# A macaron block on one core: the feed-forward bias by accumulating DMA instead of GpSimd adds

## The chip, the cores and the metric

The kernel runs on one core of a Trainium2 chip. A core has five engines with an instruction queue each: TensorE (PE, matmuls; PEld is its weight load), VectorE (DVE), ScalarE (ACT), GpSimd (POOL) and SyncE (SP), which here only issues transfers. Each queue is worked through in order; engines wait for each other through semaphores. Sixteen DMA engines move data between DRAM and the on-chip memory SBUF, whichever queue has issued the transfer. The metric is the device time of one execution in microseconds; less is better.

## What is computed

The input x has 2 sequences of 1024 rows of 1024 numbers, float32. A block runs over it: half a feed-forward network, causal attention with 32 query and 8 key/value heads of 32, and half a feed-forward network again, each on the layer-normalised rows and each added to x:

```
x = x + 0.5 * ffn(layernorm(x))
x = x + attn(layernorm(x))
x = x + 0.5 * ffn(layernorm(x))

def ffn(x):
    w_full = softmax over the 2 largest of 8 gate logits x @ gate_w.T, 0 elsewhere
    result = einsum('bsd,od->bso', x, base_w) + base_b
    low = einsum('bsd,erd->ebsr', x, lora_A)
    lora_out = einsum('ebsr,eor,bse->bso', low, lora_B, w_full)
    return result + 2.0 * lora_out
```

What matters here is `base_b`: a vector of 1024 numbers, half of which is added to every row of x twice, once in each of the two networks. Both networks have the same weights.

## The kernel before, in words

**Tiles.** The 2048 rows are 16 tiles of 128 rows. A tile of x, named xt, is 128 x 1024 float32, 512 KB in SBUF, one row to a partition. It is loaded once (L126), changed in place by both networks and the attention, and stored (L748, L750). Every dense product is made of three float16 products, high by high, high by low and low by high parts (L358 to L360), 512 columns of output at a time, in one of two PSUM buffers named pd.

**Stages of one tile.** `stage_a1` is the first network, `stage_a2` the keys, values and queries, `unit_s1` and `unit_s2` the attention of one group of heads (L573 score matmuls for the row maxima L590, then L712 scores, L718 exponentials, L636 sums of pairs, L657 products with the values), `stage_c1` the output projection, `stage_c2` the second network. Before each dense stage `layernorm` makes the normalised tile xn (L349, ScalarE), splits it into the halves hl (L310, L311), and transposes them through DMA into tt (L314). Queries are transposed by DMA too (qt, L553), twice for each pair of groups. The weights of the attention stay in DRAM as prepared halves and are streamed, 1 MB per load, into three buffers ws (L370); the weights wb of the networks stay in SBUF.

**The network** (`ffn`, L390) does this for its tile: 24 matmuls of gate and low-rank input into psa; two GpSimd adds (L395), one for each half of the columns, of the bias tile bb to xt; gate logits and routing in small VectorE steps (L400 to L418); then for each half of 512 columns 24 base matmuls, three low-rank matmuls (L440 to L442), and one VectorE instruction (L444) that scales the PSUM and adds it to xt. The two adds have to come after xn has been made, which reads xt without the bias, and before L444 of the same columns. `layernorm` also uses GpSimd, for two instructions on one number per row (L335, L337).

**The bias tile.** bb is 128 x 1024 float32 in SBUF. One SyncE transfer in the preparation (L793) reads the 4 KB of the bias once for every partition, and ScalarE halves it (L233).

**Order.** The preparation, up to about 130 us, is written out by hand: loads, scales (`pow2`, with a GpSimd power at L177), splits, and the first networks of tiles 0 to 2. `pin` keeps its SyncE transfers in program order. After it, dense work and attention are interleaved by `step` according to `plan`: in a usual step the second network of tile s-2, the output projection of s-1, keys and queries of s+1, the first network of s+2. Tile 8 (`LATE`) does its attention last, so its second network is the end of the kernel. Apart from pinned transfers, the order on each engine is laid out by a scheduler with a timeline of its own when the kernel is built, by the dependencies and by when operands are expected.

Of the kernel before, what the change touches and what calls it, by code (L numbers as in the profile page):

```python
# [9 lines left out]
FP = mybir.dt.float32  # L10
# [3 lines left out]
ALU = mybir.AluOpType  # L14
AX = mybir.AxisListType

B, T, D = 2, 1024, 1024
NH, NKV, DH, GRP = 32, 8, 32, 4
E, R = 8, 16
P = 128  # L20
KB = D // P
# [18 lines left out]
def kernel(  # L40
# [16 lines left out]
    nc = tc.nc  # L57
# [3 lines left out]
    const = ctx.enter_context(tc.tile_pool(name="const", bufs=1))  # L61
    wres = ctx.enter_context(tc.tile_pool(name="wres", bufs=1))
    small = ctx.enter_context(tc.tile_pool(name="small", bufs=SB))
# [4 lines left out]
    dram = ctx.enter_context(tc.tile_pool(name="dram", bufs=1, space=bass.MemoryType.DRAM))  # L68
# [17 lines left out]
        out=cmask, in_=cmask, compare_op=ALU.is_ge, fill=-NEG, base=0,  # L86
# [6 lines left out]
        out=tri, in_=tri, compare_op=ALU.is_gt, fill=0.0, base=0,  # L93
# [7 lines left out]
    nc.gpsimd.memset(ones, 1.0)  # L101
    cosT = const.tile([P, TPB, DH // 2], FP)
    sinT = const.tile([P, TPB, DH], FP)
    bb = const.tile([P, D], FP)

    qst = [stat.tile([P, NH, P], HP, name=f"qst{j}") for j in range(2)]
    kst = stat.tile([P, NKV, P], HP)
# [9 lines left out]
    def pin(ins):  # L117

        if pinned[0]:
            tc.keep_in_program_order(ins)  # L120
# [3 lines left out]
    def load_x(t):  # L124
        xt = xp.tile([P, D], FP, name="xt")
        pin(nc.sync.dma_start(out=xt, in_=late["x"] if t == LATE and late else xf[bass.ts(t, P), :]))  # L126
        xts[t] = xt
# [97 lines left out]
    def prep_lora(st):  # L225
        c = const.tile([P, 2], FP, name="sl")
        nc.vector.tensor_copy(c[:, 0:1], S["l",])
        nc.vector.scalar_tensor_tensor(c[:, 1:2], INV["b", 0], S["l",], S["b", 1], ALU.mult, ALU.mult)
        for n in range(2):
            h, s = bass.ts(n, 512), c[:, n : n + 1]  # L230
            nc.scalar.activation(lbh[:, h], st[:, h], AF.Copy, scale=s)
            nc.vector.scalar_tensor_tensor(lbl[:, h], st[:, h], s, lbh[:, h], ALU.mult, ALU.subtract)
        nc.scalar.mul(bb, bb, 0.5)  # L233

    KV = [wk_in, wv_in]
    CHUNKS = {
# [8 lines left out]
    def stage(ci, h, slot, eng):  # L245
        staged[ci, h] = piece(slot, CHUNKS[ci][0], h, eng)
# [81 lines left out]
    def layernorm(xt, n=1):  # L328
        st = small.tile([P, 2, 6], FP, name="bst")
        for c in range(2):  # L330
            nc.vector.bn_stats(st[:, c, :], xt[:, bass.ts(c, 512)])
        mv = small.tile([P, 2], FP, name="mv")
        nc.vector.bn_aggr(mv, st.rearrange("p a b -> p (a b)"))
        ve = small.tile([P, 1], FP, name="ve")
        nc.gpsimd.tensor_scalar(ve, mv[:, 1:2], EPS, None, ALU.add)  # L335
        r = small.tile([P, 1], FP, name="r")
        nc.gpsimd.tensor_tensor(r, ve, mhalf, ALU.pow)  # L337
        n1 = small.tile([P, 1], FP, name="n1")
        nc.vector.scalar_tensor_tensor(n1, ve, r, r, ALU.mult, ALU.mult)
        nc.vector.tensor_scalar(n1, n1, -0.5 * XS, 1.5 * XS, ALU.mult, ALU.add)  # L340
        rs = small.tile([P, 1], FP, name="rs")
        nc.vector.tensor_tensor(rs, n1, r, ALU.mult)
        nb = small.tile([P, 1], FP, name="nb")
        nc.vector.scalar_tensor_tensor(nb, mv[:, 0:1], -1.0, rs, ALU.mult, ALU.mult)
        xn = fpool.tile([P, D], FP, name="xn")
        sp = Split(n)
        for i in range(n):
            c = bass.ts(i, D // n)
            nc.scalar.activation(xn[:, c], xt[:, c], AF.Identity, bias=nb, scale=rs)  # L349
            sp.add(xn)  # L350
        return sp

    def dense(ps, tt, wsel, n=512, last=True):

        for k in range(KB):
            wh, wl = wsel(k)
            th, tl = tt.high(k), tt.low(k)
            nc.tensor.matmul(ps, lhsT=th, rhs=wh, start=(k == 0), stop=False)  # L358
            nc.tensor.matmul(ps, lhsT=th, rhs=wl, start=False, stop=False)  # L359
            nc.tensor.matmul(ps, lhsT=tl, rhs=wh, start=False, stop=(last and k == KB - 1))  # L360
            if k % 2 == 1:
                yield
# [27 lines left out]
    def ffn(xt, tt, done):  # L390
        psa = p_dense.tile([P, 512], FP, name="pd")
        yield from dense(psa[:, 0 : P + E], tt, lambda k: (ag[:, 0, k, :], ag[:, 1, k, :]))
        for n in range(2):
            c = bass.ts(n, 512)
            nc.gpsimd.tensor_tensor(xt[:, c], xt[:, c], bb[:, c], ALU.add)  # L395

        lg = small.tile([P, E], FP, name="lg")
        nc.scalar.activation(lg, psa[:, P : P + E], AF.Copy, scale=S["cg"])
        nv = small.tile([P, 1], FP, name="nv")
        nc.vector.tensor_reduce(nv, lg, AX.X, ALU.max, negate=True)  # L400
        ex = small.tile([P, E], FP, name="ex")
        nc.scalar.activation(ex, lg, AF.Exp, bias=nv)
        fe = lg.unsqueeze(1).to_broadcast([P, E, E])
        ee = lg.unsqueeze(2).to_broadcast([P, E, E])
        lw = small.tile([P, E, R], FP, name="lw", bufs=1)
        gt, eq = lw[:, :, 0:E], lw[:, :, E : 2 * E]
        nc.vector.tensor_tensor(gt, fe, ee, ALU.is_gt)
        nc.vector.tensor_tensor(eq, fe, ee, ALU.is_equal)
        nc.vector.tensor_tensor(eq, eq, tri, ALU.mult)
        nc.vector.tensor_tensor(gt, gt, eq, ALU.add)  # L410
        rk = small.tile([P, E], FP, name="rk")
        nc.vector.tensor_reduce(rk, gt, AX.X, ALU.add)
        nc.vector.scalar_tensor_tensor(ex, rk, 1.5, ex, ALU.is_lt, ALU.mult)
        sm = small.tile([P, 1], FP, name="sm")
        nc.vector.tensor_reduce(sm, ex, AX.X, ALU.add)
        nc.vector.reciprocal(sm, sm)
        nc.vector.tensor_scalar(ex, ex, sm, S["inva2"], ALU.mult, ALU.mult)
        nc.vector.tensor_tensor(  # L418
            lw, psa[:, 0:P].rearrange("p (e r) -> p e r", r=R),
            ex.unsqueeze(2).to_broadcast([P, E, R]), ALU.mult,  # L420
        )
        yield True
        psb = [None, None]
        lh = ll = None
        for n in range(2):
            ps = p_dense.tile([P, 512], FP, name="pd")
            psb[n] = ps
            yield from dense(
                ps, tt, lambda k: (wb[:, n, 0, k, :], wb[:, n, 1, k, :]), last=False
            )  # L430
            if n == 0:
                pst = p_s1.tile([P, GRP, P], FP, name="s1")[:, 0, :]
                nc.tensor.transpose(pst, lw.rearrange("p e r -> p (e r)"), ident)
                lh = small.tile([P, P], HP, name="lh", bufs=LB)
                ll = small.tile([P, P], HP, name="ll", bufs=LB)
                nc.scalar.copy(lh, pst)
                nc.vector.tensor_tensor(ll, pst, lh, ALU.subtract)
                yield
            c = bass.ts(n, 512)
            nc.tensor.matmul(ps, lhsT=lh, rhs=lbh[:, c], start=False, stop=False)  # L440
            nc.tensor.matmul(ps, lhsT=lh, rhs=lbl[:, c], start=False, stop=False)
            nc.tensor.matmul(ps, lhsT=ll, rhs=lbh[:, c], start=False, stop=True)  # L442
            yield
            nc.vector.scalar_tensor_tensor(xt[:, c], ps, S["uf", n], xt[:, c], ALU.mult, ALU.add)  # L444
            done(n)
            if n == 0:
                yield True

    def stage_a1(t):
        tt = layernorm(xts[t])  # L450
        yield

        def done(n):
            if n == 1:
                Ts["x2", t] = layernorm(xts[t])
                if t == LATE:
                    late["x"] = dram.tile([P, D], FP, name="xlate")
                    nc.sync.dma_start(out=late["x"], in_=xts.pop(t))

        yield from ffn(xts[t], tt, done)  # L460
        yield True
# [310 lines left out]
    for h in range(2):  # L772
        for src, c in ((a_in, slice(0, P)), (g_in, slice(P, P + E))):
            pin(
                nc.sync.dma_start(
                    out=agst[:, h, :, c],
                    in_=src[h * (D // 2) : (h + 1) * (D // 2), :].rearrange("(k p) n -> p k n", p=P),
# [4 lines left out]
    pin(nc.sync.dma_start(out=lst, in_=lb_in))  # L782
    b0 = [piece(h - 2, [wb_in[:, 0:512]], h, nc.sync) for h in range(2)]
    load_x(1)
    a1 = [stage_a1(t) for t in range(3)]
    next(a1[0])
    prep_gate(gst)
# [2 lines left out]
    prep_base(0, b0)  # L790
    load_x(2)
    next(a1[1])
    pin(nc.sync.dma_start(out=bb, in_=bias_in.partition_broadcast(P)))  # L793
    stage(2, 0, 0, nc.scalar)
    stage(2, 1, 1, nc.scalar)
    prep_base(1, b1)
    prep_lora(lst)
    stage(3, 0, 2, nc.sync)
    stage(3, 1, 5, nc.sync)
# [240 lines left out]
```

## Time and profile before

| | us |
|---|---|
| three runs of the kernel before: median | 1523.7 |
| lowest and highest of them | 1520.88 and 1530.89 |
| the profiled execution, in all | 1528.72 |
| its span, first to last instruction | 1527.0 |

The page of a profile gives, for one execution, the busy time of each engine, the same in 40 slices of equal length (38 us here; each digit is the busy share in tenths), the DMA queues, the chain of work that ended last, and the costliest groups of instructions. A group's line has line, engine and operation, output and input with shapes and count, then busy time and mean of one, then the engine's idle time just before them and what ended it. The chain is followed back from the last instruction, at each step to what released it: its shares say which engine or transfer ended the waits, not how busy each was. Queries of the trace give the instructions in order of time, the minimum, median and maximum of one line, what waited for what, and the sums over chosen windows.

### The profile page before, as it was taken

What the parts mean: (1) busy time and instruction counts of PE and PEld (TensorE: products, weight loads), DVE (VectorE), ACT (ScalarE), POOL (GpSimd) and SP (SyncE); (2) the same over time, 40 slices, a digit from 0 to 9 for tenths busy, and PEclk for the clock granted to TensorE, in tenths of its full rate; (3) what the DMA queues carried; (4) which work ended last, traced back from release to release, by engine and by line L of the source; (5) the groups of instructions that cost most, each with busy time, mean ns of one, the idle gap of its engine ahead of it and who ended that gap; (6) DMA issues with size and microseconds to landing.
All of it is one profiled execution on the core that took longest, in us unless ns stands there. A gap on an engine that the chain in (4) does not pass through costs nothing.

```text
span 1527.0 us, 35303 instructions
## 1 busy us (share of the span) xinstructions
PE 1404.1 (92%) x14548; PEld 783.4 (51%) x14548; DVE 1139.7 (75%) x2420; ACT 755.5 (49%) x1374; POOL 450.1 (29%) x665
## 2 busy tenths in 40 slices
PE   3686897989999999999999899999999999989998
PEld 2243444455555555555654445555555555556544
DVE  6877656686968879789764767886869788689753
ACT  7564334453545545456552434553545455556631
POOL 3443213432323233122121323332323232312231
PEclk9798999989999999999999999999999999999999
DMA  9957697658575581853646769857383853834651
GB/s 274 333 156 204 115 237 205 206 127 264 123 238 137 153 254 31 235 160 69 209 160 191 216 161 272 202 160 234 72 294 69 237 147 70 271 69 98 133 170 45
DMA packets 293075, 267.30 MB, mean 175 GB/s; under 512 B 258480, under 2 KB 261552, under 8 KB 272432
## 3 DMA queue, kind: packets, MB, share of 16 engines
q1 hardware_dynamic: 289360, 252.45, 60.5%
q10 hardware_dynamic: 3552, 12.58, 2.3%
q8 instruction: 114, 1.87, 0.5%
q14 instruction: 49, 0.40, 0.1%
HBM read 181.63 MB, written 20.45 MB: 132 GB/s over the span
## 4 chain that ended last, share of the span: by engine, by line
PE 65%; DVE 13%; DMA 13%; ACT 3%; issue 2%; POOL 1%; SPq 1%; DVEq 0%; ACTq 0%; POOLq 0%
PE pd L358 13%; PE pd L359 13%; PE pd L360 13%; PE av L657 10%; PE s L712 7%; PE s L573 6%; DMA ws<-wstr 6%; DMA qt<-qst 5%; DVE mx L590 3%; DVE pair L636 1%; DVE ws L195 1%; DMA tt<-hl 1%; DVE o L666 1%; ACT p L718 1%; DVE hl L311 1%
## 5 line engine op out<-in xcount | busy, mean ns | idle before, releaser
L718 ACT ACTIVATE p<-s,cs 128x512 f32<-128x512 f32 x576 | 382.3, 688 | 291.2 <-PE s L712 284.1
L590 DVE TENSOR_REDUCE mx<-s 128x4 f32<-128x512 f32 x480 | 313.6, 675 | 68.3 <-PE s L573 46.8
L358 PE MATMUL pd<-ws,tt 128*128 128x512 f16 x592 | 226.8, 383 | 20.9 <-DMA ws<-wstr 16.8
L636 DVE TENSOR_TENSOR pair<-p,p 128x512 f32<-128x512 f32 x256 | 185.6, 727 | 72.6 <-ACT p L718 34.8
L573 PE MATMUL s<-kts,qt 96*128 96x128 f16 x2304 | 217.0, 222 | 23.8 <-DMA qt<-qst 17.8
L359 PE MATMUL pd<-ws,tt 128*128 128x512 f16 x592 | 226.3, 382 | 0.0
L712 PE MATMUL s<-qt,kts 128*128 128x512 f16 x576 | 210.7, 386 | 16.4 <-DMA qt<-qst 11.6
L360 PE MATMUL pd<-ws,tt 128*128 128x512 f16 x592 | 225.4, 382 | 0.0
L573 PEld LDWEIGHTS <-qt 96*128 96x128 f16 x2304 | 165.5, 99 | 116.4 <-issue 30.4
L359 PEld LDWEIGHTS <-tt 128*128 128x128 f16 x1360 | 135.6, 100 | 141.9 <-issue 31.3
L358 PEld LDWEIGHTS <-tt 128*128 128x128 f16 x1360 | 135.6, 100 | 135.5 <-issue 16.7
L358 PE MATMUL pd<-wb,tt 128*128 128x512 f16 x512 | 199.0, 389 | 5.0 <-DVE xt L444 5.0
L360 PEld LDWEIGHTS <-tt 128*128 128x128 f16 x1360 | 135.3, 99 | 131.5 <-issue 10.2
L359 PE MATMUL pd<-wb,tt 128*128 128x512 f16 x512 | 198.0, 387 | 0.5 <-DVE wb L195 0.5
L360 PE MATMUL pd<-wb,tt 128*128 128x512 f16 x512 | 197.7, 386 | 0.0
L657 PE MATMUL av<-p,va 128*32 128x128 f32 x4608 | 166.8, 278 | 4.8 <-ACT o L664 2.5
L720 POOL TENSOR_SCALAR_AFFINE_SELECT p<-p 128x512 f32<-128x512 f32 x128 | 89.0, 698 | 274.7 <-ACT p L718 264.4
L673 POOL TENSOR_TENSOR tt<-o,tt 128x128 f16<-128x128 f32 x128 | 70.5, 551 | 279.6 <-ACT tt L672 279.3
L657 PEld LDWEIGHTS av<-p,va 128*32 128x32 f32 x4608 | 115.5, 110 | 68.3 <-issue 53.4
L666 DVE RECIPROCAL o<-o 128x128 f32<-128x128 f32 x128 | 120.6, 942 | 24.9 <-ACT o L664 24.9
L585 POOL TENSOR_SCALAR_AFFINE_SELECT sm<-sm 128x512 f32<-128x512 f32 x96 | 66.4, 692 | 203.9 <-ACT sm L584 202.1
L395 POOL TENSOR_TENSOR xt<-xt,bb 128x512 f32<-128x512 f32 x64 | 92.3, 1464 | 59.6 <-ACT xn L349 59.4
(177 smaller groups left out, 1808.2 us busy)
## 6 DMA issues: line engine op xcount, KB each, us to landing
ws<-wstr SPq DMA_DIRECT2D x148, 1024.0 KB, 5.9
wstr<-ws ACTq DMA_DIRECT2D x9, 1024.0 KB, 6.1
xt<-in_x_dram SPq DMA_DIRECT2D x16, 512.0 KB, 3.8
out_dram<-xt SPq DMA_DIRECT2D x15, 512.0 KB, 2.8
ws<-in_wb_dram SPq DMA_DIRECT2D x2, 1024.0 KB, 8.0
qst<-in_wb_dram SPq DMA_DIRECT2D x2, 1024.0 KB, 6.8
st<-in_wo_dram SPq DMA_DIRECT2D x2, 1024.0 KB, 10.0
kts<-in_wo_dram SPq DMA_DIRECT2D x2, 1024.0 KB, 12.0
```

The lines of the kernel that those rows point to most:

```text
L358: nc.tensor.matmul(ps, lhsT=th, rhs=wh, start=(k == 0), stop=False)
L359: nc.tensor.matmul(ps, lhsT=th, rhs=wl, start=False, stop=False)
L360: nc.tensor.matmul(ps, lhsT=tl, rhs=wh, start=False, stop=(last and k == KB - 1))
L395: nc.gpsimd.tensor_tensor(xt[:, c], xt[:, c], bb[:, c], ALU.add)
L573: nc.tensor.matmul(ps[:, h, :], lhsT=q[0 : 3 * DH, h, :], rhs=KT[b0 + j][0 : 3 * DH, g, :], start=(not pem or h == 0), stop=not pem,)
L590: nc.vector.tensor_reduce(mx[:, odd, j, :], ps, AX.X, ALU.max)
L636: nc.vector.tensor_tensor(sums, us[i][1], us[i + 1][1], ALU.add)
L657: prev = nc.tensor.matmul(av[rows, i, :], lhsT=w, rhs=p32[:, h, :], start=(us[0][0] == 0 and n == 0), stop=(last and n == len(runs) - 1), ...
L666: nc.vector.reciprocal(rc, rc)
L712: ins = nc.tensor.matmul(ps.rearrange("p h k -> p (h k)"), lhsT=KT[b0 + j][:, g, :], rhs=q.rearrange("p h k -> p (h k)"), start=True, stop ...
L718: nc.scalar.activation(p32, ps, AF.Exp, scale=cs)
L720: nc.gpsimd.affine_select(out=p32, in_=p32, compare_op=ALU.is_ge, fill=0.0, base=0, pattern=[[0, GRP], [1, P]], channel_multiplier=-1,)
```

## The change

The bias is halved once, as 4 KB laid over 128 partitions of 8 numbers, and written to a row hb in DRAM. The two adds of each network become one transfer issued by GpSimd. It reads hb for every one of the 128 partitions, and the DMA engines add what they read to xt. The tile bb, its load and its scaling by ScalarE are gone. There are 32 such transfers, two for each of the 16 tiles.

```diff
-    bb = const.tile([P, D], FP)
...
-        nc.scalar.mul(bb, bb, 0.5)
...
     def ffn(xt, tt, done):
         psa = p_dense.tile([P, 512], FP, name="pd")
         yield from dense(psa[:, 0 : P + E], tt, lambda k: (ag[:, 0, k, :], ag[:, 1, k, :]))
-        for n in range(2):
-            c = bass.ts(n, 512)
-            nc.gpsimd.tensor_tensor(xt[:, c], xt[:, c], bb[:, c], ALU.add)
+        nc.gpsimd.dma_start(out=xt, in_=hb.partition_broadcast(P), accum_op=ALU.add)
...
     load_x(1)
+    hs = small.tile([P, KB], FP, name="hs", bufs=1)
+    pin(nc.sync.dma_start(out=hs, in_=bias_in.rearrange("(p k) -> p k", k=KB)))
+    nc.gpsimd.tensor_scalar(hs, hs, 0.5, 0.0, ALU.mult, ALU.add)
+    hb = dram.tile([D], FP, name="hb")
+    nc.gpsimd.dma_start(out=hb.rearrange("(p k) -> p k", k=KB), in_=hs)
     a1 = [stage_a1(t) for t in range(3)]
...
-    pin(nc.sync.dma_start(out=bb, in_=bias_in.partition_broadcast(P)))
```

## The prediction, made before the changed kernel was built or run

> **What bounds the kernel now.** I read the page first: the busy shares, the 40 slices, the chain that ended last, then the group of the adds.
>
> ```profile
> PE 1404.1 (92%) x14548; PEld 783.4 (51%) x14548; DVE 1139.7 (75%) x2420; ACT 755.5 (49%) x1374; POOL 450.1 (29%) x665
> DMA  9957697658575581853646769857383853834651
> PE 65%; DVE 13%; DMA 13%; ACT 3%; issue 2%; POOL 1%; SPq 1%; DVEq 0%; ACTq 0%; POOLq 0%
> L395 POOL TENSOR_TENSOR xt<-xt,bb 128x512 f32<-128x512 f32 x64 | 92.3, 1464 | 59.6 <-ACT xn L349 59.4
> ```
>
> TensorE carries 65% of the chain, VectorE and DMA 13% each, GpSimd 1%. The adds are 92.3 us of an engine that the end of the kernel hardly asks for. So the change can earn little by freeing GpSimd itself; it can earn through VectorE and lose through DMA. Both were looked at closer. First VectorE's instructions in order of time where the first three tiles' six adds run (44.1 to 52.5 us):
>
> ```profile
> 44.37 2.10 DVE L311 TENSOR_TENSOR hl<-xn,hl 128x1024 f16<-128x1024 f32 x1
> 46.46 1.21 DVE L407 TENSOR_TENSOR lw<-lg 128x64 f32<-128x64 f32 x1
> 47.59 1.30 DVE L408 TENSOR_TENSOR lw<-lg 128x64 f32<-128x64 f32 x1
> 48.81 0.74 DVE L444 SCALAR_TENSOR_TENSOR xt<-pd,uf,xt 128x512 f32<-128x512 f32 x1
> ...
> L407 DVE TENSOR_TENSOR lw<-lg x32: 204/213/1212, 31.5 to 1511.7; 128x64 f32<-128x64 f32 x32
> L311 DVE TENSOR_TENSOR hl<-xn,hl x48: 1160/1221/2272, 14.7 to 1503.0; 128x1024 f16<-128x1024 f32 x48
> ```
>
> A comparison of 64 columns takes 213 ns in the median and 1212 ns beside an add: VectorE stands still while GpSimd reads SBUF. Then the DMA engines, in the 5 us after an add (columns: window, busy of PE, PEld, DVE, ACT, POOL, granted clock, DMA share, GB/s), and the landing times (the first line is that of the qt transposes, L553):
>
> ```profile
> 232.00:237.00 5.00, 3.91 (x35) 2.32 (x34) 2.70 (x3) 2.43 (x5) 3.91 (x5) 1.00 1.00 285
> 470.00:475.00 5.00, 5.00 (x47) 2.39 (x40) 3.69 (x5) 2.60 (x5) 5.00 (x5) 1.00 1.05 273
> 970.00:975.00 5.00, 5.00 (x34) 2.63 (x33) 4.52 (x7) 2.96 (x6) 5.00 (x6) 1.00 1.01 317
> 1182.00:1187.00 5.00, 5.00 (x47) 2.53 (x43) 4.96 (x7) 3.47 (x7) 5.00 (x5) 1.00 0.44 80
> ...
> DMA to landing us min/median/max: 3.0/3.9/16.4
> ...
> ws<-wstr SPq DMA_DIRECT2D x148, 1024.0 KB, 5.9
> xt<-in_x_dram SPq DMA_DIRECT2D x16, 512.0 KB, 3.8
> bb<-in_bias_dram SPq DMA_DIRECT2D x1, 512.0 KB, 4.9
> ```
>
> Of the 29 places behind the first three tiles, 10 have a DMA share of 0.99 or more in that window (232, 299, 304, 381, 470, 607, 851, 925, 970, 1144 us); the other 19 lie mostly at 0.4 to 0.7. In the stages from 200 to 400 and 800 to 1200 us the chain's largest wait is the streamed weights, 16.9% and 9.3%.
>
> **Removed.** (a) 64 adds, 92.3 us of GpSimd: beside TensorE's work, so nothing by itself. (b) VectorE's standstill. Over every VectorE instruction that overlaps an add I summed what it takes above the median of its own shape elsewhere: 28.7 us. Of this 4.7 us lie between 44.4 and 52.5 us (L311 0.9, L407 1.0, L408 1.1, L409 0.4, L410 0.5, L171 0.8), where the chain runs through exactly these instructions: all counted. The other 24.0 us I count with VectorE's share of the chain, 13%: 3.1. Gain 7.8 us, with bounds 4.7 and 28.7. (c) The 512 KB load of bb and its scaling (L233, 1.05 us of ScalarE beside VectorE's work). Its 128 packets took 315 ns each in the full stage at 35.9 us, that is 8 x 0.315 = 2.5 us of each of the 16 engines.
>
> **Added: 32 accumulating transfers** of 128 rows x 4 KB. Let D be the time for which one holds the 16 DMA engines. No row shows one. The nearest is the plain 512 KB store or load: 163 ns for a 4 KB packet in a quiet stage, 8 per engine, 1.3 us. The Trainium skill (DMA: Bandwidth & Descriptors, section "SDMA does more than copy") describes the add in the data path as an elementwise reduction of two streams: the tile has to be read as well as the row. With one stream D is 1.3, with two 2.6, and the sum below becomes +1.6 or +11.2 us. The rule speaks against the change, and I take its 2.6, because the destination must be read to be added to. The low bound is 1.3 (added traffic cannot be a gain); the high one is two streams at the 315 ns of the bias load, 5.0 us: it too reads one 4 KB row for all 128 partitions.
>
> What D costs:
> - First three tiles: 3D = 7.8 us of engine time enter a stage whose DMA share is 0.8 to 1.05, the bias load's 2.5 leave. The chain there is half transfers and half VectorE at most: half of 5.3, +2.7.
> - Streamed weights, at the 10 places with full DMA engines: the load behind an accumulation comes D later; TensorE feels it if that load ended its wait, which by the chain it did in 17% of the time from 200 to 400 us: 10 x 0.17 D = 1.7 D = +4.4 (low bound 0; 10 D if every load were on the path).
> - Transposes, everywhere. The trace shows what another queue's large packets do to them: from 137.4 to 150.8 us two qt transposes (2048 packets of 256 bytes; as many of a tt take 2.6 us alone, from 128.9 to 131.5) took 13.4 us, while a store from ScalarE's queue with 16 packets of 442 ns per engine, 7.1 us, went between them. That is 10.8 us later, about 1.5 times what the other transfer holds; for the landing of a qt the row is 3.9 us in the median and 16.4 at most, 12.5 or 1.75 times, and I use this. An accumulation comes from a third queue in the same way. The qt and kts transposes have 147,456 packets of 18 ns: 166 us of each engine, 11% of the span; TensorE's waits ended with 22 of the 128 qt, 17%. With 29 accumulations: 29 x 0.11 x 0.17 x 1.75 D = 0.9 D. The tile's own tt, 2.5 to 4 us after xn, meets it about every other time; 5 of the 48 ended a wait, 10%: 29 x 0.5 x 0.10 x 1.75 D = 2.5 D. The queue behind a late transpose (SyncE's, with the weights) I put at as much again as the qt part, 0.8 D. Together 4.2 D = +10.9, between 0 and, if every fifth late transpose stops TensorE instead of every tenth, 8 D.
>
> **Added: issue and waits.** GpSimd writes the descriptors: between 0.33 us (a plain issue by SyncE) and the 2.9 us of the two adds; about 1 us, an estimate from the first-byte latency of this path in the same page's "Specifications". In all cases GpSimd's queue gets shorter at these places, and what follows there (the mask of p L720, the mask of sm L585) is not later: nothing. The issue waits for xn (L349) as the adds do. L444 now waits for the landing, in VectorE's in-order queue, with the maxima L590 and pair sums L636 behind it, for which the score matmuls wait. Landing is about 3.8 + 1.3 + 1 = 6 us (bounds 3.1, the fastest plain x load, and 16.4, the slowest qt transpose). An add that met VectorE took 2258 ns, not 1261; if descriptor writing is stopped in the same way, landing is 7. The skill (SBUF — State Buffer, "Who interferes with whom") lets it be stopped by VectorE's two-port modes, not by two-input instructions, so it would say 6; by either, from an add to its tile's L444 I find 20 us at the least (tile 8: 1501.9 to 1521.9) and mostly 25 to 87, so nothing waits. In the prologue the add need no longer wait for bb; it can go 20 us before the 48.8 at which L444 starts.
>
> **Moved: preparation.** hs, 4 KB, goes on SyncE's queue behind x of tile 1, where SyncE is idle from 6.1 to 16.0 us; its issue (0.5 us) is free, and the bias issue of 0.58 us at 34.5 is gone. On GpSimd come one scaling (0.2 us, by L213), one 4 KB store, and the wait of the first accumulation for that store. If GpSimd takes the scaling before the power at L177 (10.4 us), it waits for the loads ahead, till about 15 us, and the gate's scale with it: up to 5 us, plus some 3 for the store. The order is the scheduler's; between 0 and 8 I take 1.
>
> **Sum** against the profiled execution (1528.7 us, span 1527.0): -7.8 + 2.7 + 1.0 + 4.4 + 10.9 = +11.2, or generally 7.4 D - 8.0. That gives 1539.9. This execution lay 5.0 us above the median of the three runs (1523.7), so 1535.
>
> **Rivals.**
> 1. *The accumulation is dear (slower; 27%).* For it: two streams, one hot row, the turns with small packets. Against: 512 KB moves in 1.4 us elsewhere. With D = 5.0 the sum is 7.4 x 5.0 - 8.0 = +29, hence 1553; with 8 D for the transposes too, 3.8 x 5.0 = 19 more, 1572. It decides from D = 3.1 us on, where 7.4 D - 8.0 passes 15 us, 1%.
> 2. *The transfer is hidden, VectorE's gain stays (28%).* D = 1.3 and streamed weights that have slack (TensorE waited only 16.8 us for them in all): -7.8 to +1.6, hence about 1520; faster by over 1% only if half of the 24 us of standstill were on the path: 4.7 + 12 = 16.7 less, 1507.
> 3. *A wait takes the place of the adds* (within the first two): landing over 20 us would stop VectorE at L444. 20 us at 32 places would be visible at once; the landing row of 3.8 us speaks against it.
> That the change doesn't do what it says would show as no GpSimd transfer in the list of issues; then nothing remains of it but the wait. I give it no chance of its own.
>
> **Numbers.** My own case has 45%: within 1% with 30, slower with 15. Rival 1: slower 25, same 2. Rival 2: faster 15, same 13. Together faster 0.15, same 0.45, slower 0.40; 1% is about what a measurement of this kernel can tell from no change. The range runs from 1506 (rival 2 with half the standstill) to 1565 (D near 5, with part of the dearer transposes); outside are the ends of both rivals, about 2 in 10.
>
> **What would show it.** L311 and L407 without their long instances, 28 us less of VectorE: step (b). The packets of the GpSimd queue: 4 KB ones at about 320 ns, D = 2.6; at 163 or above 600 the price is wrong. Waits of TensorE for ws and qt, 46 us now, near 60, and late tt: the price of contention. VectorE idle before L444 because of a transfer: the slack is wrong. The first L444 later than 48.8: the preparation. Wrong altogether I would be if descriptor writing held GpSimd for more than the adds did, or if the scheduler laid out the engines' order anew.

## The result and the profile after

| | before | after |
|---|---|---|
| median of 20 runs each (us) | 1522.4 | 1515.7 |
| lowest and highest (us) | 1513.4 and 1530.9 | 1507.5 and 1524.2 |
| profiled execution, in all (us) | 1528.7 | 1515.2 |

The changed kernel takes 0.9954 of the time before, with a 95% interval of 0.9936 to 0.9972: 0.5% faster. The forecast was 0.75% slower (1535 us); the time lies in the range of 1506 to 1565 us, the sign is wrong. Single runs of one kernel lie up to 1.2% apart here, and the profile of before comes from a long one (the spans differ by 13.6 us, 1527.0 to 1513.4, where the medians differ by 6.7), so sizes below come from medians, and profiles serve for where a wait lies.

From the page of after: busy shares, DMA slices, the queue of the new transfers (packets, MB, share of the 16 engines' span), the chain that ended last, and two groups of DMA issues.

```profile
PE 1399.4 (92%) x14548; PEld 782.4 (52%) x14548; DVE 1113.2 (74%) x2420; ACT 752.3 (50%) x1373; POOL 386.0 (26%) x635
DMA  9969497958497682864666879859386873944652
...
q0 software_dynamic: 4640, 16.78, 6.8%
...
PE 72%; DMA 11%; DVE 9%; ACT 3%; issue 2%; POOL 1%; SPq 1%; ACTq 0%; POOLq 0%; DVEq 0%
...
ws<-wstr SPq DMA_DIRECT2D x148, 1024.0 KB, 6.0
xt<-hb POOLq DMA_DIRECT2D x32, 512.0 KB, 7.2
```

VectorE is busy for 26.5 us less (1139.7 to 1113.2), nearly all of the 28.7 us of standstill, and its share of the chain falls from 13% to 9%. The new queue holds the 16 engines for 6.8% of the span: 0.068 x 1513.4 / 32 = 3.2 us for one accumulation. In the records 4,096 of its packets have 4 KB, and they take 327 ns at the least and 328 in the median: twice the 163 ns of a plain 4 KB packet in a quiet stage. The mean is 400 ns.

The new line and the two that stood still before, from the views of single lines (minimum, median and maximum in ns, first and last start in us):

```profile
L391 POOL DMA_DIRECT2D xt<-hb x32: 887/952/966, 19.8 to 1488.4; - x32
...
DMA to landing us min/median/max: 5.1/7.2/19.4
...
L403 DVE TENSOR_TENSOR lw<-lg x32: 203/214/756, 35.9 to 1498.0; 128x64 f32<-128x64 f32 x32
...
L309 DVE TENSOR_TENSOR hl<-xn,hl x48: 1195/1223/3282, 14.1 to 1489.3; 128x1024 f16<-128x1024 f32 x48
```

Writing descriptors takes GpSimd 0.95 us per network. The comparisons of 64 columns have lost their 1.2 us instances. All 32 transfers land within 20 us, and in the view of L440, the scaled addition behind them (L444 before), no wait for a DMA is listed.

### The profile page after: what moved, and what is told of

Its sections match the earlier page's. It is cut to its first block, busy times and chain, and to the rows that moved or that the text cites. A ratio compares the mean times of both kernels' runs of the same rounds, so it can differ in the third digit from the quotient of the medians.

```text
span 1513.4 us, 35332 instructions
## 1 busy us (share of the span) xinstructions
PE 1399.4 (92%) x14548; PEld 782.4 (52%) x14548; DVE 1113.2 (74%) x2420; ACT 752.3 (50%) x1373; POOL 386.0 (26%) x635
## 4 chain that ended last, share of the span: by engine, by line
PE 72%; DMA 11%; DVE 9%; ACT 3%; issue 2%; POOL 1%; SPq 1%; ACTq 0%; POOLq 0%; DVEq 0%
PE pd L356 14%; PE pd L357 14%; PE pd L358 14%; PE av L653 12%; PE s L569 7%; PE s L708 7%; DMA ws<-wstr 4%; DMA qt<-qst 4%; DVE mx L586 2%; DMA st<-in_wv_dram 1%; DVE pair L632 1%; ACT p L714 1%; DMA tt<-hl 1%; DVE o L662 1%; DVE ws L194 1%
## 5 line engine op out<-in xcount | busy, mean ns | idle before, releaser
L569 PE MATMUL s<-kts,qt 96*128 96x128 f16 x2304 | 219.6, 221 | 30.0 <-DMA qt<-qst 26.2
L356 PE MATMUL pd<-ws,tt 128*128 128x512 f16 x592 | 226.8, 383 | 15.6 <-DMA ws<-wstr 14.7
L569 PEld LDWEIGHTS <-qt 96*128 96x128 f16 x2304 | 164.5, 98 | 126.8 <-issue 31.2
L632 DVE TENSOR_TENSOR pair<-p,p 128x512 f32<-128x512 f32 x256 | 177.1, 694 | 68.5 <-ACT p L714 24.7
L358 PE MATMUL pd<-ws,tt 128*128 128x512 f16 x592 | 226.2, 383 | 0.0
L708 PE MATMUL s<-qt,kts 128*128 128x512 f16 x576 | 210.3, 385 | 7.8 <-DMA qt<-qst 4.8
L358 PEld LDWEIGHTS <-tt 128*128 128x128 f16 x1360 | 135.5, 100 | 135.1 <-issue 13.8
L356 PEld LDWEIGHTS <-tt 128*128 128x128 f16 x1360 | 135.7, 100 | 132.8 <-issue 12.9
L356 PE MATMUL pd<-wb,tt 128*128 128x512 f16 x512 | 198.1, 387 | 3.3 <-DVE t L466 1.6
L358 PE MATMUL pd<-wb,tt 128*128 128x512 f16 x512 | 197.3, 385 | 0.0
L669 POOL TENSOR_TENSOR tt<-o,tt 128x128 f16<-128x128 f32 x128 | 63.9, 500 | 303.2 <-ACT tt L668 303.1
L580 ACT COPY sm<-s 128x512 f32<-128x512 f32 x96 | 55.9, 583 | 72.4 <-PE s L569 66.9
```

Of the source, the lines that this page charges most:

```text
L569: nc.tensor.matmul(ps[:, h, :], lhsT=q[0 : 3 * DH, h, :], rhs=KT[b0 + j][0 : 3 * DH, g, :], start=(not pem or h == 0), stop=not pem,)
L632: nc.vector.tensor_tensor(sums, us[i][1], us[i + 1][1], ALU.add)
L708: ins = nc.tensor.matmul(ps.rearrange("p h k -> p (h k)"), lhsT=KT[b0 + j][:, g, :], rhs=q.rearrange("p h k -> p (h k)"), start=True, stop ...
```

## The experiments

Two effects were argued in the forecast, the standstill and the traffic, and a third was set to nothing: the scheduler orders the instructions anew. To keep these apart, some kernels below are laid out by the scheduler exactly as before or after, and only then are chosen bias instructions cut to 2 columns. Every instruction keeps its place and its waits. The ratios are to the kernel before, run beside them on the same chip, with their 95% intervals. The edited copies keep the line numbers of before; in the changed kernel the same lines stand two or four higher (L356 for L358, L569 for L573, L708 for L712).

**1. The adds cut in the order of before.**

```diff
-            nc.gpsimd.tensor_tensor(xt[:, c], xt[:, c], bb[:, c], ALU.add)
+            BIAS.append(nc.gpsimd.tensor_tensor(xt[:, c], xt[:, c], bb[:, c], ALU.add).ins.name)
...
+    def cut(i):
+        def few(p):
+            return _copy.replace(p, ap=[list(p.ap[0]), [1, 2]], bass_ap=None)
+        return _copy.replace(i, ins=[few(p) for p in i.ins], outs=[few(p) for p in i.outs])
+    for fn in nc.m.functions:
+        for bl in fn.blocks:
+            bl.instructions = [cut(i) if i.name in BIAS else i for i in bl.instructions]
```

> The kernel before, every engine in the order in which it was laid out, but each of the 64 adds of GpSimd is cut to 2 of its 512 columns, so the bias is left out of the others. That takes away the standstill of VectorE (28.7 us) and GpSimd's 92 us, adds no transfer and moves nothing. If the gain of the change is the standstill, and the transfers cost nothing on the path: ratio to before about 0.995, the same as the change. If the prediction's step was right and only 7.8 us come from it: 0.995 too, but then the transfers must cost little or the order must have paid for them. If the gain came with the new order of the engines: 0.998 or more.

Measured: 1502.1 us, 0.9869 (0.9846 to 0.9893). The full adds cost some 20 us of the end, not 8.

**2. The accumulations cut in the order of after.** The same edit, on the transfer.

```diff
-        nc.gpsimd.dma_start(out=xt, in_=hb.partition_broadcast(P), accum_op=ALU.add)
+        BIAS.append(nc.gpsimd.dma_start(out=xt, in_=hb.partition_broadcast(P), accum_op=ALU.add).ins.name)
```

> The changed kernel, every engine in its order, each accumulating transfer cut to 2 of 1024 columns: the bias is left out of the others. That takes away the traffic (102 us of the 16 engines), and leaves issue, waits and order. If the traffic is hidden: the same as the changed kernel, within 2 us. If the prediction's price of the traffic was right (5.9 D with D = 3.2 us, some 19 us) and something else paid for it: 0.983 or less.

Measured: 1490.1 us, 0.9798 (0.9772 to 0.9824).

**3. The changed kernel again**, beside these two, with no edit.

> The changed kernel itself, beside the two above on one chip: 0.995, as measured. It is the reference for the small transfers.

Measured: 1517.0 us over 22 runs, 0.9967 (0.9949 to 0.9986). The data of the accumulations thus cost 1517.0 - 1490.1 = 27 us in this order.

**4. No bias at all**: adds, tile, load and scaling taken out before the layout.

```diff
-    bb = const.tile([P, D], FP)
...
-        nc.scalar.mul(bb, bb, 0.5)
...
-        for n in range(2):
-            c = bass.ts(n, 512)
-            nc.gpsimd.tensor_tensor(xt[:, c], xt[:, c], bb[:, c], ALU.add)
...
-    pin(nc.sync.dma_start(out=bb, in_=bias_in.partition_broadcast(P)))
```

> The bias left out altogether: no adds, no bias tile, no transfers; the order is laid out anew. If standstill is the gain and the traffic is hidden: the same as the changed kernel, 0.995 (0.993 to 0.997). If the traffic costs what the prediction said: below 0.985. If the order decides: anything, apart from the small adds.

Measured: 1501.9 us, 0.9865 (0.9838 to 0.9892), as with the cut adds. With the 1523.3 us of the kernel before beside them, runs 1 to 4 split the result: from 1523.3 to 1502.1 without the adds' data (-21), from there to the new order without its data 1490.1 (-12), and with the data 1517.0 (+27). The sum is -6. Each part is a difference of two medians, good to some 3 or 4 us; by the ratios the parts are -20, -11 and +26. That a third order without any bias takes 1502 shows that leaving work out does not by itself make the 12 us. What is left between runs 1 and 2 is the order, with 64 adds of two columns in one and 32 small transfers in the other; "the order" below means all of that.

TensorE's waits in the order of before, first with whole adds (run 8, whose bias is zero; span 1511.6 us) and then with cut adds (waiter, what it waited for, us in all, times, longest):

```profile
PE s L573 <- DMA qt<-qst: 16.6, 8, 6.3
PE pd L358 <- DMA ws<-wstr: 13.4, 12, 2.2
PE s L433 <- DVE lw L418: 12.0, 6, 3.7
PE s L712 <- DMA qt<-qst: 10.6, 11, 2.2
```

```profile
PE s L573 <- DMA qt<-qst: 17.6, 8, 5.4
PE s L712 <- DMA qt<-qst: 12.7, 12, 2.2
PE pd L358 <- DMA ws<-wstr: 10.4, 10, 2.2
...
PE s L433 <- DVE lw L418: 5.4, 4, 3.0
```

All waits of TensorE for VectorE, summed over this view, fall from 53.0 to 40.2 us, the spans by 15.4. About half of the fall is the routing weights (lw, 12.0 to 5.4): short VectorE steps that run beside the adds, and TensorE waits for their end.

The same view for the order of after, first with the accumulations cut and then whole:

```profile
PE pd L358 <- DMA ws<-wstr: 11.9, 11, 2.6
...
PE s L573 <- DMA qt<-qst: 8.9, 10, 1.9
PE s L712 <- DMA qt<-qst: 8.8, 7, 3.1
```

```profile
PE s L569 <- DMA qt<-qst: 26.2, 10, 13.8
PE pd L356 <- DMA ws<-wstr: 14.7, 10, 3.0
...
PE s L708 <- DMA qt<-qst: 4.8, 4, 3.1
```

In the order of before 30.3 us of waits for qt remain without the adds' data (17.6 + 12.7); in the order of after 17.7. The 12 us of the order may lie here, but it is not shown: the spans of these two profiles differ by 2.6 us only (1496.2 and 1493.6), and TensorE is busy for 6.1 us longer in the second (1391.3 and 1397.4). With the data of the accumulations the waits for qt are 31.0 us in this profile and 26.5 in that of run 3.

One path is not separated in these runs, the clock granted to TensorE. Its mean over the executions is 0.975 before, 0.981 in run 1, 0.982 in run 2 and 0.975 in run 3. Over the 27 executions of the kernel before, the time is 1.4 us shorter for each 0.001 of clock; by this estimate some 8 of the 20 us of run 1 go with the higher clock, and a like share of the 27. No run tells whether shorter waits raise the clock. The cut data start it either way, since nothing else was changed.

**5. Standstill or GpSimd's time?** The adds of before, in their places, become powers of 4 numbers per row from a constant. They hold GpSimd and read next to nothing.

Against run 1, where a is the constant 0.5 as 4 numbers per row and o the first 4 columns of the output:

```diff
-        return _copy.replace(i, ins=[few(p) for p in i.ins], outs=[few(p) for p in i.outs])
...
+        return _copy.replace(i, op=ALU.pow, ins=[a, a], outs=[o])
```

> The kernel before in its order, each of the 64 adds replaced by a power of 4 numbers per row: GpSimd is busy for a like time (about 1 to 2 us each, to be read from the profile), but hardly reads SBUF. It leaves the bias out and overwrites 4 columns of each half of x with a constant. If the 20 us that the small adds gained are VectorE's standstill: about as fast as those, 0.987 to 0.989. If they are GpSimd's own time, as its queue delays what stands behind the adds: near 1.0.

Measured: 1506.9 us, 0.9893 (0.9873 to 0.9913). The lines of the powers and of the routing comparison:

```profile
L395 POOL TENSOR_TENSOR xt<-half x64: 1002/1017/1961, 44.0 to 1480.8; 128x4 f32<-128x4 f32 x64
```

```profile
L407 DVE TENSOR_TENSOR lw<-lg x32: 206/212/517, 31.8 to 1489.6; 128x64 f32<-128x64 f32 x32
```

GpSimd is held for 65 us in all (by the adds 92), and the comparison has lost its 1.2 us instances; 16 of the 21 us are still won. So the standstill carries most of the gain. The other 5 us (1506.9 - 1502.1) would be GpSimd's own time, but the intervals of runs 1 and 5 overlap, so they are not told from nothing.

**6. Only the first six adds cut** (first three tiles, preparation). Against run 1:

```diff
+        seen.append(i.name)
+        if not (len(seen) <= 6):
+            return i
```

> The kernel before in its order, only the first six adds (the first networks of the first three tiles, 44 to 52 us) cut to 2 columns, so the bias is left out there. The prediction counted 4.7 us for these. By the profiles of the kernel before and of the small adds the gain at the third L444 was 6.6 us and grew to 14 by 173 us without further adds but four. If the preparation carries it all: 6 to 14 us, 0.991 to 0.996. If it is given back in the transfers behind: 0.998 or more.

Measured: 1518.7 us, 0.9967 (0.9952 to 0.9983), 4.5 to 5 us. This is the 4.7 of the forecast.

**7. The ten adds from 108 to 307 us cut.** The condition is `7 <= len(seen) <= 16`.

> The kernel before in its order, only the ten adds between 108 and 307 us cut to 2 columns (the bias is left out there). Cutting the first six gained 5 us, cutting all 64 gained 20; 15 lie in the other 58. By their standstill (8.4 of the 24 us behind the preparation) these ten would carry 5 to 6 us: 0.996 to 0.997. If the stage with full DMA engines hides what VectorE loses there: 0.999. If that stage carries nearly all: 0.991.

Measured: 1521.1 us, 0.9980 (0.9955 to 1.0005), not told from nothing; 2 us by the medians. Summed once more from the trace of before, the standstill is 4.7 us until 60 us, 5.2 from there to 310, and 18.8 behind it; the 8.4 in the expectation was too much. By difference the 48 adds behind 310 us cost 20 - 5 - 2 = 13 us, good to some 5. They were not cut alone.

**8. Bias of zeros**, the adds whole: `nc.scalar.mul(bb, bb, 0.0)` in place of 0.5.

> The kernel before, with a bias tile scaled by 0 in place of 0.5: all work is done, with the numbers that the kernels with cut adds have. If the numbers themselves do nothing to the time: 1.000 within 0.002. If they did (through the granted clock), the gains of the cut kernels would have to be read against this one.

Measured: 1520.4 us, 0.9993 (0.9972 to 1.0013). The numbers in x, which several of these kernels change, do not move the time by more than this interval allows, about 4 us.

**9. Where do the 12 us of the order come from: the load of the bias?** Run 1, with the load of bb and its scaling cut as well.

```diff
-        nc.scalar.mul(bb, bb, 0.5)
+        BIAS.append(nc.scalar.mul(bb, bb, 0.5).ins.name)
...
-    pin(nc.sync.dma_start(out=bb, in_=bias_in.partition_broadcast(P)))
+    ld = nc.sync.dma_start(out=bb, in_=bias_in.partition_broadcast(P)); pin(ld); BIAS.append(ld.ins.name)
```

> The small adds in the order of the kernel before, and in addition the load of the bias tile and its scaling cut to 2 columns (the bias is left out but for 2 columns of each half). The small transfers lay 12 us under the small adds (1490.1 to 1502.1); between them stand the 512 KB load in the full preparation and the order of the engines. If it is the load: 0.980 to 0.983. If it is the order: 0.987, as the small adds.

Measured: 1503.7 us, 0.9879 (0.9849 to 0.9909), the same as run 1 within the intervals. No cost of the load's data shows.

**10. Or the time at which the bias is there?** The kernel before with bb loaded behind x of tile 1 and scaled at once, laid out anew.

```diff
-        nc.scalar.mul(bb, bb, 0.5)
...
     load_x(1)
+    pin(nc.sync.dma_start(out=bb, in_=bias_in.partition_broadcast(P)))
+    nc.scalar.mul(bb, bb, 0.5)
...
-    pin(nc.sync.dma_start(out=bb, in_=bias_in.partition_broadcast(P)))
```

> The kernel before, all by GpSimd adds, but the bias tile loaded behind x of tile 1 and scaled at once, so that the adds of the first three tiles can go some 20 us earlier; order laid out anew, no accumulating transfer. If the 12 us between the two orders come from the bias being there early: 0.990 to 0.995 with the adds still paid. If they come from elsewhere: 0.996 to 1.003.

Measured: 1524.7 us, 1.0006 (0.9983 to 1.0029). That is not it either.

**11. Two accumulations alone.** Between the profiles of runs 2 and 3, which have one order, the starts of the same instructions lie 8 us apart at 255 us and 15 at 326, measured on TensorE's instructions. Here only the seventh and eighth accumulation are cut, issued at 281.5 and 285.6 us. Against run 2:

```diff
+        seen.append(i.name)
+        if not (7 <= len(seen) <= 8):
+            return i
```

> The changed kernel in its order, only the seventh and eighth accumulation (281.5 and 285.6 us, in the stage where a qt transpose made TensorE wait 13.8 us) cut to 2 columns; the bias is left out there. If the traffic's price is this one collision: 8 to 13 us faster than the changed kernel, 0.989. If it is spread over all 32: 2 us, 0.995.

Measured: 1506.7 us, 0.9893 (0.9871 to 0.9915): 10 of the 27 us sit at this one place. The timeline of SyncE's queue (start, duration, what), first after, then with the two cut, where both kernels are alike up to 283.7 us:

```profile
283.74 10.66 SPq L312 DMA_TRANSPOSE tt<-hl  x1
294.50 0.52 SPq L368 DMA_DIRECT2D ws<-wstr  x1
295.12 14.25 SPq L549 DMA_TRANSPOSE qt<-qst  x3
```

```profile
283.82 5.37 SPq L314 DMA_TRANSPOSE tt<-hl  x1
289.30 0.52 SPq L370 DMA_DIRECT2D ws<-wstr  x1
289.91 7.26 SPq L553 DMA_TRANSPOSE qt<-qst  x3
```

And TensorE at the end of it, in the changed kernel (in brackets the wait before the instruction and who ended it):

```profile
294.73 0.65 PE L653 MATMUL av<-pair,ones 128*32 128x128 f32 x8
309.13 1.46 PE L569 MATMUL s<-kts,qt 96*128 96x128 f16 x12 [13.75 <-DMA qt<-qst]
```

While two accumulations and the streamed weights share the engines, the transposes take twice as long, 10.66 for 5.37 us and 14.25 for 7.26, and the second of them starts late besides. TensorE stands for 13.8 us; with the two cut, its longest wait for a qt in this stretch is 1.6. The size of the wait varies: in the profile of run 3, the same kernel, the two transposes take 10.13 and 9.83 us and TensorE stands for 9.1. It also runs slower at this place, first in the changed kernel, then with the two cut (the columns are those of the windows in the prediction; the third from the end is the granted clock):

```profile
293.00:313.00 20.00, 6.23 (x70) 5.10 (x71) 3.73 (x6) 2.85 (x6) 0.63 (x1) 0.50 1.19 167
```

```profile
293.00:313.00 20.00, 18.43 (x230) 13.13 (x231) 13.67 (x31) 8.13 (x18) 3.96 (x7) 0.78 0.56 153
```

Twelve score matmuls (L569) take 1.46 us at 309 us, and 0.84 us at 320 us, where the granted clock is 1.00 again. So not all of the 10 us need be the wait itself. In the records the 4 KB packets of the second accumulation run from 290.3 to 304.7 us, 727 ns each in the mean; the one at 380.8 us, at 328 ns a packet, is through in 2.6 us.

**12. Only the first three accumulations whole.** In run 11's edit the condition is `len(seen) > 3`.

> The changed kernel in its order, only the first three accumulations whole, the other 29 cut to 2 columns (the bias is left out there). All 32 cut gained 27 us, two of them alone 10. By the profiles the first three put the first L444 back by 4 us: then 1494 to 1497, 0.981 to 0.983. If traffic in the preparation is hidden behind TensorE's later work: 1490, 0.979; if it carries what is not in the two: 1506, 0.989.

Measured: 1498.0 us, 0.9830 (0.9795 to 0.9865). The first three cost 1498.0 - 1490.1 = 8 us by the medians and 5 by the ratios (0.9830 and 0.9798), the other 29 the remaining 19 to 21: 10 or 11 at the place of run 11 and some 9 at the other 27.

**13. Transfers for the first three networks, adds for the rest**, laid out anew.

```diff
+        nff[0] += 1
+        if nff[0] <= 3: nc.gpsimd.dma_start(out=xt, in_=hb.partition_broadcast(P), accum_op=ALU.add)
+        else: [nc.gpsimd.tensor_tensor(xt[:, bass.ts(n, 512)], xt[:, bass.ts(n, 512)], bb[:, bass.ts(n, 512)], ALU.add) for n in range(2)]
```

> Accumulating transfers for the first networks of the first three tiles alone, GpSimd adds with the bias tile for the other 29; order laid out anew. By the runs so far: 5 us gained (standstill), 3 to 5 given back (traffic in the preparation, with the tile's load still there): 0.997 to 1.001. If the order in the preparation carries a gain of its own: below 0.993.

Measured: 1519.4 us, 0.9973 (0.9956 to 0.9991), a gain of 4 us. It has an order of its own, so it cannot be split into the parts above.

**14. Is the one row in DRAM what makes a packet dear?** The source of the accumulation is a bias tile in SBUF, loaded and scaled as before.

```diff
-        nc.gpsimd.dma_start(out=xt, in_=hb.partition_broadcast(P), accum_op=ALU.add)
+        nc.gpsimd.dma_start(out=xt, in_=bb, accum_op=ALU.add)
```

> The changed kernel with the bias tile in SBUF as the source of the accumulation, loaded and scaled as in the kernel before; no row in DRAM. If the price of 327 ns for 4 KB is that of two streams through the engine, packets stay at 327 ns and the time at 0.995 to 0.999, with the load's cost on top. If it is the one row that all 128 partitions read in DRAM: packets nearer 163 ns, and 10 us faster than the changed kernel, 0.989.

Measured: 1540.6 us, 1.0115 (1.0089 to 1.0142). Its packets take 327 ns at the least and 336 in the median: the row in DRAM is not at fault. Two streams fit the doubled time; a cost of the adding itself was not told apart from them. The kernel is slower for another reason. Its first three accumulations wait for the tile, run together from 48.6 to 66.2 us, and VectorE meets one of them (the view of L444: the idle time before it, and then the wait of TensorE behind it):

```profile
L444 DVE SCALAR_TENSOR_TENSOR xt<-pd,uf,xt x64: 651/745/753, 58.6 to 1531.8; 128x512 f32<-128x512 f32 x64
...
  DMA xt<-bb: 6.0, 1
```

```profile
PE pd L358 <- DVE xt L444: 9.3, 3, 8.5
```

The first L444 starts at 58.6 us, in the changed kernel at 45.3. If this delay lasts to the end, it is 13 of the 24 us between the two kernels; the rest was not traced.

**15. The two dear accumulations back on GpSimd.** The changed kernel, with the bias tile loaded from hb behind the preparation, and adds for the second network of tile 1 and the first of tile 5.

```diff
+        if key not in BYADD: nc.gpsimd.dma_start(out=xt, in_=hb.partition_broadcast(P), accum_op=ALU.add)
+        else: [nc.gpsimd.tensor_tensor(xt[:, bass.ts(n, 512)], xt[:, bass.ts(n, 512)], bb[:, bass.ts(n, 512)], ALU.add) for n in range(2)]
...
     load_x(4)
+    nc.sync.dma_start(out=bb, in_=hb.partition_broadcast(P))
```

> The changed kernel, but the two networks whose accumulations met the qt transpose (the second network of tile 1 and the first of tile 5) go back to GpSimd adds, from a bias tile loaded after the preparation. The cut of these two gained 10 us in the order as it was; two pairs of adds bring back some 1 to 3 us of standstill. If the order that is laid out anew is no worse: 0.989 to 0.992, faster than both kernels. If the collision moves to another place: 0.995.

Measured: 1510.7 us, 0.9917 (0.9888 to 0.9947): faster than before, and by the medians 5 to 6 us faster than the changed kernel, which was not run beside it. Its interval and that of run 3 (0.9949 to 0.9986) just do not overlap.

## Why the prediction was wrong

**Step (b) failed, and the order had no price.** Step (b) says: "The other 24.0 us I count with VectorE's share of the chain, 13%: 3.1." Runs 1, 6 and 7 put the adds behind the preparation at 15 us: 20 for all, 5 for the preparation, the rest by difference, of which 13 for 18.8 us of standstill behind 310 us. By run 5 some 11 of the 15 are standstill; the rest may be standstill too, or GpSimd's own time, step (a), which was counted as nothing. The share of the chain says how much of the end VectorE's own work makes up. It does not say how much slack lies behind a certain instruction. The adds come while the gate logits are routed, and for the routing weights TensorE waits. The bound of 28.7 was in the text; the likeliest value was taken far below the middle, from an average over stages. The part of (b) in the preparation, read from the instructions there, was right.

**The order was priced at nothing.** It stood in the last sentence as what would make the forecast wrong, with no number. It is worth 11 or 12 us here. That the new order was the shorter one was luck, so far as the runs go: the bias load and its time were tried and are not the cause, and which of the many exchanged places is the cause stays open.

**The traffic was under-sized**, 26 to 27 us for 2.7 + 4.4 + 10.9 = 18.0. The quiet price, D = 2.6, was right (328 ns packets); 3.2 is the mean. With it the terms of the streamed weights and the transposes give (1.7 + 4.2) x 3.2 = 18.9 us for the 29 later places, where 19 were measured. The agreement is partly chance: the sum was spread evenly over 29 places, and half of it fell on one. Also, the 17% for the streamed weights was read from 200 to 400 us, where only four of the ten places lie; four lie in the stage with 9.3%. The first three, put at 2.7, cost 5 to 8. The row that was used for the transposes (another queue's packets lengthen them) held in kind: they took up to twice as long.

**Right were** the 28 us less of VectorE (26.5), the issue of about 1 us (0.95), a landing of 6 to 7 us (7.2), and that no L444 waits for it. TensorE's waits for qt and ws were to go from 46 to near 60. They stayed at 46 (26.2 + 4.8 + 14.7 = 45.7), in the profile of run 3 at 41 (20.1 + 6.4 + 14.3 = 40.8). In the profiles of runs 1 and 2 they are 40.7 (30.3 + 10.4) and 29.6, so the traffic gave back what was less in the new order.

**Together:** the adds 12 us more gain, the order 12 more, the traffic 9 more loss: from +11 to about -4, where the medians show -6. Rival 2 had the sign by the wrong half: its standstill came true, but its transfer was not hidden. Rival 1's point of decision, D = 3.1, was passed in the mean, and the gains that it left out outweighed it.

## What to carry to other kernels

Price the stopping of an engine from the stage in which it stops, by who waits for the instruction just then; its share of the chain is no measure of that. A change of operations also changes the order that a scheduler lays out, and this alone was worth 0.7 to 0.8% here; to measure the operation, keep the order and cut the instruction's data after the layout. The new transfer cost most where two of them met streamed weights and small-packet transposes, so look for such a place before judging the whole.

## What the hardware showed beyond that

An accumulating 4 KB packet takes 327 ns, twice 163, whether its source is one row in DRAM or a tile in SBUF. This agrees with the two streams of the Trainium skill (DMA: Bandwidth & Descriptors, "SDMA does more than copy"), though no run tells their reading from the adding. A GpSimd power of 4 numbers per row holds GpSimd for 1.0 us and lets VectorE's comparisons take 517 ns at most, while an add of 512 columns, 1.26 us when it met no VectorE work, stopped a VectorE instruction for 1.0 us. Other work of GpSimd seems to stop VectorE too. In the profile of after one split (L309) took 3.3 us for its usual 1.2, with no add of the bias left; beside it ran three GpSimd instructions, two of them two-input ones for the queries:

```profile
121.70 0.95 POOL L471 TENSOR_TENSOR t<-qs,sinT 128x256 f32<-128x256 f32 x1
122.39 0.94 POOL L475 TENSOR_TENSOR t<-qs,sinT 128x256 f32<-128x256 f32 x1
123.10 0.89 POOL L191 TENSOR_SCALAR ws<-st,s_o 128x512 f16<-128x512 f32 x1
```

```profile
121.79 3.28 DVE L309 TENSOR_TENSOR hl<-xn,hl 128x1024 f16<-128x1024 f32 x1 [0.19 <-ACT hl L308]
```

That these stopped it is read from their times, 121.70 to 123.99 us; they were not cut.
